# A convolution, an MLP and a scan on one core: the first stage's head and tail, its rows in DRAM, and the MLP's PSUM banks

## The chip, the core and the metric

The kernel runs on one core of a Trainium2 chip. Its time is device microseconds, the median of several runs. The profile is that of one execution. Engines are named as in the profile: PE multiplies matrices, DVE and ACT are the vector and scalar engines, POOL is GpSimd, SP only issues DMAs. ACT and POOL issue DMAs too.

## The reference

The input x is 32 images of 96 channels, 56 x 56, float32. Layer 0 is a depthwise 7x7 convolution, a LayerNorm over channels, a two-layer MLP with gelu, a scale and the residual. Layer 1 is a depthwise 5x5 convolution with silu and then a scan along the 3136 pixels. Cut to what matters:

```python
# layer 0
h = depthwise_conv7x7(x, conv_w) + conv_b           # then channels last
h = (h - mean(h)) * rsqrt(var(h) + 1e-5) * ln_g + ln_b
h = gelu(h @ w1 + b1) @ w2 + b2                      # 96 -> 384 -> 96
x = h * layer_scale + x
# layer 1
xs = silu(depthwise_conv5x5(x, conv_w) + conv_b)     # (B, 96, 3136)
dts, Bs, Cs = split(x_proj_w @ xs)                   # 6, 4, 4 rows
delta = softplus(dt_w @ dts + dt_b)
dA = maximum(delta * A, log(1e-9));  P = exp(cumsum(dA))
hs = P * cumsum(delta * Bs * xs / maximum(P, 1e-9))
y = einsum(hs, Cs) + xs * Ds
```

## The kernel before

The stages run one after the other on the core: the first convolution with the sums for the LayerNorm (0 to about 387 us of the profiled execution), the MLP with the residual (to about 1210), the second convolution (to about 1560) and the scan.

**First convolution.** There are 48 jobs. Each takes four pairs of a channel and a half of the image's rows (jobs 0 to 39: two channels, both halves; 40 to 43: four channels, upper half h = 0; 44 to 47: the lower half). `load_x(n)` brings a job's input `xt` in four DMAs of 224 KB, `load_taps(n)` its taps `wt` in four DMAs of 28 KB from `taps1_d`, a padded copy of the taps in DRAM that DVE builds in `pad` and a DMA stores first. `turn(n)` copies `wt` on ACT into one of three banded matrices `mats`. `convolve(n)` is 128 matmuls (line 380) into two of the four PSUM buffers of the pool `c1_ps`, each of two banks. `evict(n)` adds the bias on ACT (L408) and stores the result to `conv1_d` from ACT's queue (L414). `add_sums(n)` adds it to the running sums `acc1` on DVE (L430 to L436), and one job later its squares (ACT L439) to `acc2` (L441).

Loads run three jobs ahead, and `xt` and `wt` have four buffers each. Between the jobs, from n = 2 on, one function of the list `beside` runs in each turn: `first_weights` (folding the LayerNorm into w1: two small matmul groups in the PSUM buffers `ps_w1` and `ps_b1`), four times `first_rows` (copies of that result into `w1r_t`), `second_weights`, `scan_weights` (another small matmul, `ps_wd`), and the taps of the second convolution. `finish_norm(h)` makes 1/std of half h of the rows in five DVE operations, a Sqrt on ACT and a reciprocal on DVE; it is called for h = 0 at job `upper` = 44, for h = 1 in the MLP. POOL's queue stores its result to `rstd_d`. `load_rows(n)` loads a group's rows for the MLP: three tiles `h` of 4 rows x 32 channels, and the matching 1/std `r`. `normalise` multiplies them.

**Order.** An instruction inside `pin(...)` keeps its place in program order on its engine; one without it may be moved by the scheduler to where it judges its inputs ready. In the built kernel before, the unpinned SP loads are reordered: the taps `wt` of jobs 6 and 7 stand ahead of the input of job 6, from then on taps run two jobs further ahead than inputs; four loads of the first `h` tile stand among the loads of the jobs near 17 and four of the second among those near 33; the second convolution's taps store (L279) stands on SP as well. DMAs issued from SP and ACT take turns on eight completion semaphores, and one that takes a semaphore waits for the DMA that used it last.

**MLP.** 28 groups of rows, two halves each (`parts` = 56). In each, `hidden` (L520, into `ps_h`, three PSUM buffers of two banks) and gelu (L530), then `result` (L539, into `ps_o`, two buffers of one bank), the residual on DVE (L553), and a store to `block_d` from POOL's queue (L564). Rows and residual inputs are loaded two groups ahead.

**Second convolution and scan.** They read `block_d` (L625) and `conv2_d`; the scan runs units of four operations on DVE (L825 to L832), three on ACT (L809 to L811) and two on POOL (L815, L844).

## Time and profile before

| | |
|---|---|
| runs, us | 3349.49, 3348.69, 3347.18 (median 3348.69) |
| profiled execution, us | 3343.99, its span 3342.2 |
| busy share of the span | PE 83%, DVE 78%, ACT 67%, POOL 50% |
| mean granted PE clock | 0.819 |
| first convolution matmul | 17.90 us |
| first MLP matmul, first gelu | 387.18 us, 393.44 us |
| DMA | 788.08 MB, 236 GB/s over the span |
| row loads h<-conv_d | 336 DMAs of 112 KB, 2.6 us to landing |

Times within the execution are from its start. A bracket after an instruction gives how long its engine had been idle before it, and what released it; "DMA wt<-taps_d" is the DMA that wrote wt from the taps in DRAM. PEld is PE's weight load; SPq, ACTq and POOLq are the issuing of DMAs by those engines. In the profile, buffer and tensor numbers are left out: `conv_d` is conv1_d in the first stage, `taps_d` is taps1_d or taps2_d.

### The profile page before, as it was taken

The page shows a single profiled execution, that of the slowest core. Times are in us where ns is not written, and L with a number is a line of the kernel's source. Part 1 is how long each engine was busy: PE and PEld are TensorE (multiplying, and loading weights), DVE is VectorE, ACT ScalarE, POOL GpSimd, SP SyncE. Part 2 cuts the span into 40 slices and gives each one's busy share as a digit, 9 for nine tenths or more (in the row PEclk, how much of TensorE's full clock was granted, in tenths as well). Part 3 has the DMA queues.
Part 4 walks back from the last instruction along what each step waited for, and adds up shares of the span by engine and source line. Part 5 has one row for each costly group of instructions (what it writes and reads, how often), then busy time and mean ns, then how long its engine had stood idle before and what let it go on. Part 6 is the DMA issues. An engine that isn't in the chain of part 4 may idle for free. (4 is left out here: it accounts for less than half of the span.)

```text
span 3342.2 us, 54129 instructions
## 1 busy us (share of the span) xinstructions
PE 2775.9 (83%) x21898; PEld 1064.9 (32%) x21898; DVE 2599.4 (78%) x1538; ACT 2241.5 (67%) x1963; POOL 1686.6 (50%) x815
## 2 busy tenths in 40 slices
PE   5999899999999989997677777777777777777775
PEld 2566433333333333343222222222222222222221
DVE  4888743333333349997799999999999999999998
ACT  3566543333333348786888887888888888878784
POOL 1000101010010100000899898989899998989896
PEclk8999899999999999998666666666666666666767
DMA  7899856555565459998887877878787878778773
GB/s 188 262 304 293 237 152 182 149 166 163 150 183 145 129 142 278 285 289 226 293 296 246 284 258 272 261 271 277 257 280 248 291 250 283 255 273 264 269 267 113
DMA packets 303130, 788.08 MB, mean 236 GB/s; under 512 B 125680, under 2 KB 195952, under 8 KB 278336
## 3 DMA queue, kind: packets, MB, share of 16 engines
q1 hardware_dynamic: 266832, 659.81, 62.9%
q10 hardware_dynamic: 27200, 82.59, 6.6%
q0 software_dynamic: 8848, 42.23, 4.5%
q8 instruction: 172, 2.82, 0.4%
q14 instruction: 78, 0.64, 0.1%
HBM read 543.58 MB, written 240.90 MB: 235 GB/s over the span
## 5 line engine op out<-in xcount | busy, mean ns | idle before, releaser
L815 POOL TENSOR_TENSOR rep<-rep,bt 128x1568 f32<-128x1568 f32 x192 | 674.5, 3513 | 380.4 <-DMA rep<-du_d 380.4
L844 POOL TENSOR_TENSOR hs<-hs,ct 128x1568 f32<-128x1568 f32 x191 | 669.4, 3505 | 98.6 <-DVE hs L832 87.2
L825 DVE TENSOR_TENSOR_SCAN pv<-rep,pv 128x1568 f32<-128x1568 f32 x192 | 664.4, 3461 | 40.0 <-ACT rep L811 23.0
L530 ACT ACTIVATE g<-ph,b1p_t 128x896 f32<-128x896 f32 x336 | 319.9, 1003 | 483.0 <-PE ph L520 483.0
L553 DVE SCALAR_TENSOR_TENSOR o<-po,b2r_t,x 128x224 f32<-128x224 f32 x336 | 190.8, 609 | 529.9 <-PE po L539 523.1
L564 POOL DMA_DIRECT2D block_d<-o x168 | 81.2, 490 | 727.5 <-DVE o L553 622.4
L520 PE MATMUL ph<-h,w1r_t 32*128 32x448 f32 x4032 | 430.2, 554 | 5.9 <-ACT hs L408 4.2
L743 PE MATMUL pz<-xs,wd_t 96*96 96x392 f32 x512 | 275.3, 703 | 172.6 <-ACT du L751 128.0
L539 PE MATMUL po<-g,w_t 128*32 128x448 f32 x4032 | 413.0, 543 | 0.0
L862 PE MATMUL py<-hs,sel_t 128*32 128x392 f32 x1536 | 324.9, 673 | 61.8 <-POOL hs L844 61.6
L790 PE MATMUL pk<-bn,pick_t 8*128 8x392 f32 x1024 | 289.0, 685 | 93.5 <-ACT y L871 80.4
L828 DVE SCALAR_TENSOR_TENSOR pv<-pv,rep 128x1568 f32<-128x1568 f32 x192 | 345.6, 1800 | 21.7 <-POOL rep L815 1.8
L380 PE MATMUL ps<-xt,mat 32*64 32x432 f32 (+2 forms) x6144 | 320.9, 564 | 45.2 <-ACT mat L362 38.4
L832 DVE TENSOR_TENSOR_SCAN hs<-rep,carry_h,pv 128x1568 f32<-128x1568 f32 x96 | 334.1, 3480 | 10.0
L660 DVE COPY st<-yt 28x896 f32<-28x896 f32 x288 | 323.3, 1123 | 22.7 <-ACT yt L651 12.7
L637 PE MATMUL ps<-xq,wt 128*32 128x448 f32 x3072 | 307.2, 546 | 38.6 <-DMA xq<-block_d 29.3
L832 DVE TENSOR_TENSOR_SCAN hs<-rep,pv 128x1568 f32<-128x1568 f32 x96 | 328.4, 3420 | 9.6
L810 ACT ACTIVATE rep<-rep,lift_t 128x1568 f32<-128x1568 f32 x192 | 307.6, 1602 | 6.2
L811 ACT ACTIVATE rep<-rep,lift_t 128x1568 f32<-128x1568 f32 x192 | 307.6, 1602 | 6.3
L809 ACT ACTIVATE rep<-rep,a_t 128x1568 f32<-128x1568 f32 x192 | 308.3, 1606 | 1.8 <-DMA rep<-du_d 1.4
L854 PE MATMUL py<-xs,dsm_t 96*96 96x392 f32 x512 | 299.7, 726 | 10.0 <-ACT ct L794 4.5
L520 PEld LDWEIGHTS ph<-h,w1r_t 32*128 32x128 f32 x4032 | 192.3, 185 | 245.5 <-issue 153.0
(110 smaller groups left out, 2795.6 us busy)
## 6 DMA issues: line engine op xcount, KB each, us to landing
rep<-du_d SPq DMA_DIRECT2D x191, 1568.0 KB, 8.2
du_d<-du SPq DMA_DIRECT2D x126, 588.0 KB, 9.2
xq<-block_d SPq DMA_DIRECT2D x192, 225.0 KB, 5.1
xt<-in_x_dram SPq DMA_DIRECT2D x192, 224.0 KB, 4.6
block_d<-o POOLq DMA_DIRECT2D x168, 240.0 KB, 4.9
h<-conv_d SPq DMA_DIRECT2D x336, 112.0 KB, 2.6
x<-in_x_dram SPq DMA_DIRECT2D x336, 112.0 KB, 2.5
conv_d<-st SPq DMA_DIRECT2D x96, 392.0 KB
```

The costliest lines, as they stand in the source:

```text
L380: nc.tensor.matmul(pss[k // 2][2 * RW * p : 2 * RW * p + 2 * RW, k % 2, :HALF].rearrange("p (i r) -> p i r", r=W2)[:, :, lo:hi], lhsT=wv[r ...
L520: pin(nc.tensor.matmul(phs[i // 2][:, i % 2, :HALF], lhsT=w1r_t[rows, d, f * 128 : (f + 1) * 128], rhs=hts[n, d][rows, s * HALF : (s + 1) ...
L530: pin(nc.scalar.activation(gt, ph[:, :, :HALF], AF.Gelu, bias=b1p_t[:, f : f + 1], scale=1.0))
L539: pin(nc.tensor.matmul(po[CB * i : CB * i + CB, :HALF], lhsT=w2_t[:, f, CB * d : CB * d + CB], rhs=gts[n, s, f, i // 2][:, i % 2], start=( ...
L660: pin(copy(st[:, :, :, :, f], yt[RW * f : RW * f + QR].rearrange("p h (b q) -> p h b q", q=QW),))
L809: pin(nc.scalar.activation(da, da, AF.Exp, scale=a_t[:, g : g + 1]))
L815: pin(nc.gpsimd.tensor_mul(ut, ut, bts[i // NG]))
L825: pin(nc.vector.tensor_tensor_scan(grown, da, zero, pv[:, last : last + 1] if q else 1.0 / EPS, ALU.mult, ALU.add))
L828: pin(nc.vector.scalar_tensor_tensor(run, in0=grown, scalar=1.0, in1=ut, op0=ALU.min, op1=ALU.mult))
L832: pin(nc.vector.tensor_tensor_scan(ht, da, run, carry_h[:, col : col + 1] if q else 0.0, ALU.mult, ALU.add))
L844: pin(nc.gpsimd.tensor_mul(ht, ht, cts[k]))
L862: pin(nc.tensor.matmul(py[g * DG : (g + 1) * DG, s, :BK], lhsT=sel_t, rhs=hss[k * NG + g][:, cols], start=False, stop=True, tile_position= ...
```

## The change

- The DRAM tensor `conv1_d` is laid out by block of 32 channels, so that a tile `h` of 4 rows x 32 channels is loaded by one DMA of 448 KB in place of four of 112 KB. `block_d` is declared with two dimensions merged; its memory is as it was.
- At the head, the taps store and the first `wt` are issued by SP instead of ACT, the store ahead of the first input; a one-element copy `warm` on ACT comes first. POOL's loads of w1, ln_g, ln_b, b1 and two small matrices come before the other parameters.
- `first_weights`, all `first_rows` and the small matmul for `wd_t` run before the first job, in one PSUM buffer.
- All loads of inputs, taps, rows and 1/std are pinned. `load_rows(0)` is called at job 44 (before: 45), `load_rows(1)` after the last job. The reciprocal of `finish_norm(0)` comes ahead of job 44's sums on DVE.
- `rstd_d` is stored through SP instead of POOL, the second taps store through POOL instead of SP.
- The MLP's two PSUM pools are opened in the other order: `ps_o` takes the first two banks, `ps_h` the other six.

In the built program PE, DVE and ACT execute the same compute instructions but for one copy more on ACT; SP's order in the first stage becomes: input of job n, taps of job n, input of job n + 1, and so on, then the 1/std store, three h tiles, four r loads, and the same for group 1.

```diff
--- before.py
+++ after.py
@@ -80,8 +80,8 @@
 
 
 
-    conv1_d = [dram.tile([128, C, HALF], F32, name=f"conv1_{h}_d") for h in range(2)]
-    block_d = dram.tile([C, H, QC, B2, BI * QP], F32, name="block_d")
+    conv1_d = [dram.tile([C // CB, 128, CB, HALF], F32, name=f"conv1_{h}_d") for h in range(2)]
+    block_d = dram.tile([C, H, QC, B * QP], F32, name="block_d")
     conv2_d = dram.tile([C, H, B * W], F32, name="conv2_d")
     du_d = dram.tile([B * NCH, C, 2, CH], F32, name="du_d")
     rstd_d = [dram.tile([128, HALF], F32, name=f"rstd_{h}_d") for h in range(2)]
@@ -139,7 +139,7 @@
         pin(nc.scalar.activation(a2, a2, AF.Sqrt, bias=eps_t, scale=1.0))
         yield
         pin(nc.vector.reciprocal(a1, a2))
-        nc.gpsimd.dma_start(rstd_d[h], a1)
+        pin(nc.sync.dma_start(rstd_d[h], a1))
         yield
 
 
@@ -158,22 +158,17 @@
         h, row, p = group(n)
         for d in range(blocks):
             ht = inputs.tile([128, COLS], F32, name=f"h_{n}_{d}", tag="h", bufs=9)
-            for i in range(RB):
-                nc.sync.dma_start(
-                    two(ht[CB * i : CB * i + CB]),
-                    conv1_d[h].rearrange("(p s m) c q -> p m c s q", s=2, m=RW)[
-                        p, row + i, CB * d : CB * d + CB
-                    ],
-                )
+            rows = conv1_d[h][d].rearrange("(p s m) c q -> p (m c) s q", s=2, m=RW)
+            pin(nc.sync.dma_start(two(ht), rows[p, CB * row : CB * (row + RB)]))
             hts[n, d] = ht
         rt = inputs.tile([128, COLS], F32, name=f"r_{n}", tag="r")
         rts[n] = rt
         for i in range(RB):
             at = rstd_d[h][2 * RW * p + row + i, 0:1]
-            nc.sync.dma_start(
+            pin(nc.sync.dma_start(
                 two(rt[CB * i : CB * i + CB]),
                 bass.AP(at.tensor, at.offset, [[0, CB], [RW * HALF, 2], [1, HALF]]),
-            )
+            ))
 
     def normalise(n, d):
         pin(nc.vector.tensor_mul(hts[n, d], hts[n, d], rts[n]))
@@ -189,19 +184,20 @@
         ]
 
         kt1 = prep.tile([C, K1, K1], F32, name="kt1")
-        nc.sync.dma_start(kt1, c1w.rearrange("c (i j) -> c i j", j=K1))
+        pin(nc.sync.dma_start(kt1, c1w.rearrange("c (i j) -> c i j", j=K1)))
         xts: dict = {}
         wts: dict = {}
 
         def load_x(n):
             xts[n] = pool.tile([128, 2 * COLS], F32, name=f"xt1_{n}", tag="xt")
             for k, (c, h) in enumerate(jobs[n]):
-                nc.sync.dma_start(
+                pin(nc.sync.dma_start(
                     two(xts[n][RW * k : RW * k + RW]),
                     x[c].rearrange("(j m) q -> m j q", m=H)[h * (H - RW) : h * (H - RW) + RW],
-                )
-
-        load_x(0)
+                ))
+
+        warm = prep.tile([128, 1], F32, name="warm1")
+        pin(nc.scalar.copy(warm, eps_t))
 
         def column(src, n, name, pool=prep):
             t = pool.tile([n, 1], F32, name=name)
@@ -217,7 +213,8 @@
         pad = prep.tile([C, TP, K1], F32, name="pad1")
         nc.vector.memset(pad, 0.0)
         nc.vector.tensor_copy(pad[:, QR : QR + K1], kt1)
-        nc.scalar.dma_start(taps1_d, pad.rearrange("c p j -> c (p j)"))
+        pin(nc.sync.dma_start(taps1_d, pad.rearrange("c p j -> c (p j)")))
+        load_x(0)
 
         mats = [prep.tile([128, SJ, RW], F32, name=f"mat_{i}") for i in range(3)]
         for t in mats:
@@ -225,25 +222,25 @@
         for t in acc1, acc2:
             nc.vector.memset(t, 0.0)
 
-        c2b_t = across(c2b, 128, C, "c2b_t", const)
-        dtb_t = column(dtb, C, "dtb_t", const)
+        w1_t = prep.tile([C, F], F32, name="w1_t")
+        nc.gpsimd.dma_start(w1_t, w1)
         g_t = column(ln_g, C, "g_t")
         lnb_t = column(ln_b, C, "lnb_t")
+        b1_t = prep.tile([128, 3], F32, name="b1_t")
+        nc.gpsimd.dma_start(b1_t, b1.rearrange("(f p) -> p f", p=128))
+        xp_t = prep.tile([R, C], F32, name="xp_t")
+        nc.gpsimd.dma_start(xp_t, xp[:R, :])
+        dtwT_t = prep.tile([R, C], F32, name="dtwT_t")
+        nc.gpsimd.dma_start(dtwT_t, dtwT)
         b2_t = column(b2, C, "b2_t")
         ls_t = column(ls, C, "ls_t")
         ls_b = across(ls, 128, C, "ls_b")
+        nc.gpsimd.dma_start(w2_t, w2.rearrange("(f p) c -> p f c", p=128))
+        c2b_t = across(c2b, 128, C, "c2b_t", const)
+        dtb_t = column(dtb, C, "dtb_t", const)
         ds_t = column(ds, C, "ds_t")
-        w1_t = prep.tile([C, F], F32, name="w1_t")
-        nc.gpsimd.dma_start(w1_t, w1)
-        b1_t = prep.tile([128, 3], F32, name="b1_t")
-        nc.gpsimd.dma_start(b1_t, b1.rearrange("(f p) -> p f", p=128))
-        nc.gpsimd.dma_start(w2_t, w2.rearrange("(f p) c -> p f c", p=128))
-        xp_t = prep.tile([R, C], F32, name="xp_t")
-        nc.gpsimd.dma_start(xp_t, xp[:R, :])
         xpT_t = prep.tile([C, R + 2 * N], F32, name="xpT_t")
         nc.gpsimd.dma_start(xpT_t, xpT)
-        dtwT_t = prep.tile([R, C], F32, name="dtwT_t")
-        nc.gpsimd.dma_start(dtwT_t, dtwT)
         for g in range(NG):
             nc.gpsimd.dma_start(
                 a_t[:, g : g + 1],
@@ -276,7 +273,7 @@
                             pad2[:, k, RW - K2 : RW, f * 2 + t], turned[:, :, j]
                         )
             if k == QC - 1:
-                nc.sync.dma_start(taps2_d, pad2)
+                nc.gpsimd.dma_start(taps2_d, pad2)
 
         w1g = prep.tile([C, F], F32, name="w1g")
         held: dict = {}
@@ -286,15 +283,18 @@
             cen = prep.tile([C, C], F32, name="cen")
             kept(nc.vector.tensor_scalar, cen, ident[:C, :C], -1.0 / C, None, ALU.add)
             kept(nc.vector.tensor_scalar, w1g, w1_t, g_t, None, ALU.mult)
-            held["w1"] = bank("ps_w1")[:, 0]
+            ps = bank("ps_w1")
+            held["w1"], ps = ps[:, 0], ps[:, 1]
             nc.tensor.matmul(held["w1"][:C, :F], lhsT=cen, rhs=w1g, start=True, stop=True)
-            ps = bank("ps_b1")[:, 0]
             for f in range(3):
                 nc.tensor.matmul(
                     ps[:, f : f + 1], lhsT=w1_t[:, f * 128 : (f + 1) * 128], rhs=lnb_t,
                     start=True, stop=True,
                 )
             kept(nc.vector.tensor_add, b1p_t, ps[:, :3], b1_t)
+
+            held["wd"] = ps[:C, 256 : 256 + C]
+            nc.tensor.matmul(held["wd"], lhsT=xp_t, rhs=dtwT_t, start=True, stop=True)
 
         def first_rows(i):
             for d in range(C // CB):
@@ -315,10 +315,6 @@
                     )
 
         def scan_weights():
-
-            ps = bank("ps_wd")[:, 0]
-            nc.tensor.matmul(ps[:C, :C], lhsT=xp_t, rhs=dtwT_t, start=True, stop=True)
-            kept(nc.vector.tensor_copy, wd_t, ps[:C, :C])
             kept(nc.vector.tensor_scalar, dsm_t, ident[:C, :C], ds_t, None, ALU.mult)
             kept(nc.scalar.activation, a_t, a_t, AF.Exp)
             kept(nc.vector.tensor_scalar, a_t, a_t, -1.0, None, ALU.mult)
@@ -342,8 +338,7 @@
                 sel_t, ident.rearrange("p (d n) -> p d n", n=N), mybir.AxisListType.X, ALU.add
             )
 
-        beside = [first_weights] + [lambda i=i: first_rows(i) for i in range(RB)]
-        beside += [second_weights, scan_weights, scan_rows, turn_taps]
+        beside = [second_weights, scan_weights, scan_rows, turn_taps]
         beside += [lambda k=k: second_taps(k) for k in range(QC)]
 
         def load_taps(n):
@@ -351,10 +346,10 @@
             wt = pool.tile([128, RW * K1], F32, name=f"wt1_{n}", tag="wt")
             for k, (c, h) in enumerate(jobs[n]):
                 at = taps1_d[c, (1 - h) * R1 * K1 : (1 - h) * R1 * K1 + 1]
-                (nc.sync if n else nc.scalar).dma_start(
+                pin(nc.sync.dma_start(
                     wt[RW * k : RW * k + RW],
                     bass.AP(at.tensor, at.offset, [[K1, RW], [1, RW * K1]]),
-                )
+                ))
             wts[n] = wt
 
         def turn(n):
@@ -409,9 +404,10 @@
                         to, ps, AF.Identity, bias=c1b_t[:, ch : ch + 1], scale=1.0
                     ))
             for g in range(2) if n < whole else [h]:
-                cs = slice(c, c + 2) if n < whole else slice(c, c + JT)
+                d, at = divmod(c, CB)
+                cs = slice(at, at + 2) if n < whole else slice(at, at + JT)
                 of = slice(2 * g, 2 * g + 2) if n < whole else slice(0, JT)
-                pin(nc.scalar.dma_start(conv1_d[g][:, cs], hs[:, of]))
+                pin(nc.scalar.dma_start(conv1_d[g][d][:, cs], hs[:, of]))
             return hs
 
         def add_sums(n, hs):
@@ -446,8 +442,12 @@
         for n in range(1, 3):
             load_x(n)
             load_taps(n)
-        for n in range(2):
-            turn(n)
+        turn(0)
+        first_weights()
+        for i in range(RB):
+            first_rows(i)
+        kept(nc.vector.tensor_copy, wd_t, held["wd"])
+        turn(1)
         upper = whole + len(jobs[whole:]) // 2
         squares = None
         for n in range(len(jobs)):
@@ -464,8 +464,8 @@
             if n == len(jobs) - 2:
                 for d in range(blocks):
                     normalise(0, d)
+            next(norm, None)
             before, squares = squares, add_sums(n, hs)
-            next(norm, None)
             if n + 2 < len(jobs):
                 turn(n + 2)
 
@@ -476,9 +476,9 @@
                 squares = None
             if n >= 2 and beside:
                 beside.pop(0)()
-            if n == len(jobs) - 3:
+            if n == upper:
                 load_rows(0)
-                load_rows(1)
+        load_rows(1)
 
 
 
@@ -487,8 +487,8 @@
     with tc.tile_pool(name="mlp_g", bufs=14) as pool_g, tc.tile_pool(
         name="mlp_ot", bufs=1
     ) as pool_o, tc.tile_pool(name="mlp_x", bufs=9) as pool_x, tc.tile_pool(
-        name="mlp_h", bufs=3, space=PSUM
-    ) as ps_h, tc.tile_pool(name="mlp_o", bufs=2, space=PSUM) as ps_o:
+        name="mlp_o", bufs=2, space=PSUM
+    ) as ps_o, tc.tile_pool(name="mlp_h", bufs=3, space=PSUM) as ps_h:
         xts: dict = {}
         gts: dict = {}
 
@@ -562,7 +562,7 @@
                 m = (1 - h) * QR + row
                 for i in range(RB):
                     nc.gpsimd.dma_start(
-                        block_d[CB * d : CB * d + CB, m + i].rearrange("c k j q -> c (k j q)"),
+                        block_d[CB * d : CB * d + CB, m + i].rearrange("c k q -> c (k q)"),
                         ot[CB * i : CB * i + CB].rearrange("p k q -> p (k q)"),
                     )
 
@@ -621,10 +621,11 @@
             wts[c] = wt
             for h in range(2):
 
-                rows = block_d[c, (H - RW + 2) * (1 - h) : (H - RW + 2) * (1 - h) + RW - 2]
+                first = (H - RW + 2) * (1 - h)
+                rows = block_d[c, first : first + RW - 2]
                 pin(nc.sync.dma_start(
                     xqs[c % len(xqs)][h][2 * QC * h : 2 * QC * h + (RW - 2) * QC],
-                    rows.rearrange("m k j q -> (m k) (j q)"),
+                    rows.rearrange("m k q -> (m k) q"),
                 ))
 
         def convolve(c):
```

## The prediction

> **What bounds the kernel now.** I read the busy times by stage first (columns: length, busy time of PE, PEld, DVE, ACT, POOL, then granted clock, DMA share, GB/s).
>
> ```profile
> 38.40:55.00 16.60, 2.58 (x11) 1.94 (x12) 8.54 (x6) 6.11 (x6) 0.00 (x0) 0.60 0.83 230
> 55.00:112.60 57.60, 50.84 (x903) 22.12 (x902) 45.20 (x49) 25.61 (x26) 0.00 (x0) 0.94 0.68 205
> 112.60:324.00 211.40, 201.09 (x3980) 142.98 (x3988) 187.87 (x125) 122.70 (x124) 0.00 (x0) 0.99 0.97 292
> 324.00:387.00 63.00, 48.75 (x894) 35.04 (x877) 54.85 (x45) 34.62 (x48) 0.55 (x1) 0.89 0.88 266
> 900.00:1000.00 100.00, 100.00 (x992) 37.43 (x988) 33.84 (x52) 38.77 (x41) 11.59 (x24) 1.00 0.61 175
> 2300.00:2700.00 400.00, 305.90 (x1080) 95.84 (x1078) 386.66 (x134) 333.18 (x282) 367.76 (x140) 0.68 0.80 264
> ```
>
> The MLP (900:1000) is bound by PE alone, the scan (2300:2700) by DVE with POOL close behind. The change alters neither's compute. Only the first convolution, up to 387 us, has an idle PE. The timeline says where (start, duration, instruction, idle time before it and its releaser):
>
> ```profile
> 15.95 1.28 ACT L362 ACT_TABLE_LOAD   x1 [15.95 <-DMA wt<-taps_d]
> 17.90 20.48 PE L380 MATMUL ps<-xt,mat 32*64 32x448 f32 x384 [17.90 <-ACT mat L362]
> 52.41 1.56 PE L290 MATMUL ps_w<-w1g,cen 96*96 96x384 f32 x2 [14.04 <-DVE w1g L259]
> 54.98 9.04 PE L380 MATMUL ps<-xt,mat 32*64 32x448 f32 x132
> ...
> 72.02 6.53 PE L380 MATMUL ps<-xt,mat 32*64 32x448 f32 x128 [1.08 <-ACT hs L408]
> ...
> 112.62 44.22 PE L380 MATMUL ps<-xt,mat 32*64 32x448 f32 x892 [0.71 <-DVE wd_t L259]
> 160.23 8.15 PE L380 MATMUL ps<-xt,mat 32*64 32x448 f32 x128 [3.39 <-ACT mat L362]
> 197.19 44.53 PE L380 MATMUL ps<-xt,mat 32*64 32x448 f32 x896 [0.38 <-ACT mat L362]
> 316.94 37.88 PE L380 MATMUL ps<-xt,mat 32*64 32x448 f32 x768 [0.25 <-ACT mat L362]
> 361.53 8.66 PE L380 MATMUL ps<-xt,mat 32*64 32x448 f32 x128 [6.71 <-ACT mat L362]
> 373.71 9.28 PE L380 MATMUL ps<-xt,mat 32*64 32x448 f32 x128 [3.52 <-ACT mat L362]
> 387.18 6.34 PE L520 MATMUL ph<-h,w1r_t 32*128 32x448 f32 x28 [4.19 <-ACT hs L408]
> ```
>
> The reader is to see three kinds of idle PE: the wait for w1g (14.04), a small wait for an eviction in every job up to 112, and waits for ACT's matrix (mat) in the middle and at the end. A job is 128 matmuls. Undisturbed it takes 44.53 x 128/896 = 6.36 us. Jobs 0 to 2 start at 17.90, job 3 at 54.98, job 10 at 112.62, job 40 at 316.94; job 47 ends at 383.0.
>
> **The change part by part.** The sum is made against the profiled execution (span 3342.2, 3343.99 in all); the median shown, 3348.69, is 4.7 us above that, so gains are subtracted from the median.
>
> A. *Head.* ACT's first copy of taps waits until 15.95 for wt, then pays a 1.28 table load. The taps store still issues at 3.4 (DVE's pad copy ends at 3.39) and still takes 4.2 us until wt 0 may issue (7.60 to 9.39). But only four x DMAs lie ahead of wt 0 on SP, not eight, and a wt took 4.0 us to land (median of the first 60 us, DMA view): 13.4; the table is loaded by then; copy 0.6: 14.0. PE first runs the weights: w1's DMA issues at 3.4 to 3.9 on POOL instead of 8.06, +6.7 (its landing row) = 10.6, w1g 0.41, then 1.56 + 1.28 + gaps 0.4 + wd 0.40 = 14.6. Job 0 starts at 14.5: gain 3.4. Bounds: 5 if wt lands in 3, a loss of 1 if w1 still lands at 15. x 0 is issued 2.6 us later (SP waits on the pad copy with x 0 behind it); with a landing of 4.3 it is there by 10, ahead of taps.
>
> B. *Jobs 2 to 3.* PE waits 14.04 for w1g, which sits in DVE's order behind the sums, and its four matmuls end at 54.98: 38.38 to 54.98 is 16.6. All leave this place. The next thing late: the matrix of job 3 was copied at 38.34, that of job 4 only at 47.58, 3 us behind need, as ACT's store issue waited for an input load. Value 15; bounds 10 and 16.6.
>
> C. *Jobs 3 to 9.* ps_w stays in one of four PSUM buffers until DVE has made all 12 copies of w1r, four turns later, so each job waits for an eviction (1.08). 57.64 us went into seven jobs; at 6.4 they take 44.8: gain 12.8. The 12 copies (0.55 each, 6.7) and wd's 0.25 now run from about 14.6 to 21.5 on DVE, which has nothing until job 0's eviction (26 before). Job 1's second buffer is that one, free at 21.5, when job 0 ends at 21: nothing to pay; without that cover 6.9.
>
> D. *Jobs 10 to 39.* 204.3 us for 30 jobs, against 192 at 6.4. The losses sit at jobs 17 to 20 (3.39 idle at 160.23, then starts 9.0, 7.6 and 7.1 apart) and 33 to 36. There SP's order held the second conv's taps store (5.0 waiting on DVE, by SP's waits) and four row loads of h each time; both leave: the store to POOL, idle then, the rows behind the last input by pins. Value 12; bounds 5 and 14.
> Here the skill speaks against the change: "DMA: Bandwidth & Descriptors", Rules for kernel authors, says to issue a DMA early and wait late, so its fixed cost overlaps. By it the early row loads were right: D would be 0 and two loads (3.1 each by that page's 2.0 us + bytes/436 GB/s, an estimate) would come to the end, about 18 us off my sum. The trace shows ACT's copy waiting 8.9 us in two waits on h<-conv_d, mid-stage, and at the end the rows are not last: 1/std is. I take the row.
>
> E. *Job 40 to the first gelu*, 316.94 to 393.44. Jobs 40 to 45 run to 354.8 as before. The matrix of job 46 stands behind the forced squares and Sqrt on ACT. Before, job 44's store issue waited until 358.66 for SP's row loads; now nothing does (SP and ACT share eight completion semaphores in program order, so a store may wait for an earlier SP load). Finish ends on DVE at 357.8, Sqrt 0.67, copy 0.6: job 46 starts at 359.0, cold, 8.7, to 367.7. Reciprocal 2.94 now precedes job 44's sums: 361.4; rstd is on SP then, with only row loads and x of the MLP behind it. It lands at 365.2 (3.8 was POOL's landing), r (2.9) by 369. Job 45's store uses a semaphore after rstd's: ACT waits until 365.2, then copies job 47's matrix at 365.8, still in time. Job 47 ends at 374. Of the two ends of this part, before:
>
> ```profile
> 358.66 0.33 ACTq L414 DMA_DIRECT2D conv_d<-hs  x1
> ...
> 368.90 3.59 SPq L173 DMA_DIRECT2D r<-rstd_d  x8
> ...
> 393.44 1.91 ACT L530 ACTIVATE g<-ph,b1p_t 128x896 f32<-128x896 f32 x2
> ```
>
> the first is the late store issue, the second the 1/std rows that SP could issue only then, with ACT's next store behind them on a shared semaphore (372.63), the third the first gelu. DVE needs to 369.8 for job 45's sum, 372 for squares, 375.2 for normalise (3.09). In the new bank order the first ph needs banks of job 46, not 47, so the 4.19 goes. ACT: evict 47, Square 46 behind DVE's sum at 379.4, 1.7, table 1.28: first gelu 382.4. Gain 11; bounds 4 and 14 (if DVE lags less).
>
> F. *Row loads in the MLP.* 336 DMAs of 112 KB become 84 of 448 KB. The same page (Anatomy of one DMA) gives a fixed 2.0 us each: 252 x 2.0 = 504 us, as an estimate. The row is PE 100.00 of 100.00 busy: h comes two turns ahead, so this is 0. What if the cover were gone: a later landing of 4.7 instead of 2.6, some 2 us once. The new row layout leaves row pieces and bytes as they are, and block_d is the same memory under other names: 0. rstd 1 on SP waits for DVE at part 5, with part 6's rows behind it, which have 29 us to spare: 0.
>
> Sum: 3.4 + 15 + 12.8 + 12 + 11 = 54.2; 3348.7 - 54.2 = 3294.5.
>
> **The rivals.**
> *DMA takes PE's place.* A job moves 0.92 MB in, 0.92 out and 0.11 of taps: 1.95 MB, 6.67 us at the 292 GB/s of 112.6:324. With DMA share 0.97 that may be the pace. Then C is 10.9 and D 4.2, B 12: 3.4 + 12 + 10.9 + 4.2 + 11 = 41.5, and with a further 10 lost in filling the queue at the head about 31: 3307 to 3318. Against: 197 to 242 ran seven jobs without an idle PE at 6.36.
> *The pinned loads wait on the stores (slower).* Before, wt ran two jobs further ahead of its input on SP. Now wt n+3 comes directly behind x n+3, and its last DMA reuses the semaphore of job n-1's store, so SP waits for that to land, and the next inputs queue behind. Loop from the end of job n-1 to job n+3: evict 1.9, issue 0.8, landing 5.4, issue 0.9, wt landing 4.9, a turn on ACT 2.7, copy 0.6: 17.2 us against three jobs, 19.1. Each 3 us over costs 1 per job. It decides where the pace passes 7.5 (48 x 7.5 + 14.5 = 374.5, plus the end's 8 gives the old 383): landings summing to 15.6 instead of 10.3 (6.9 of the loop is other work). At 17 the loop is 23.9, the pace 8.0, job 47 ends at 48 x 8.0 + 22.5 = 406.5: 24 us slower, 3372. Against: the medians, under a DMA share of 0.97.
> *It doesn't do what it says at the head*: weights land as late as before, PE's in-order queue then holds job 0 to 20: 5.5 less, 3300, inside the main case.
>
> **How the numbers follow.** Main case (gain 42 to 66) 0.68; DMA pace or a partial loss (gain 7 to 42) 0.22; within 0.2% (6.7 us, about what a measurement of this kernel tells from no change) 0.03; slower 0.07. Predicted 3294.5. The low end, 3278, is a gain of 70: the upper bounds of A, B, D and E with C make 62.4, and a pace 0.2 us shorter over the 37 jobs of C and D, 7.4 more (320 to 340 us held 418 matmuls in 20.00 busy us: 6.12 a job). The high end, 3320, takes in the DMA case (gain 29); the slow case and partial losses beyond stay outside, about 0.15 with the tail below.
>
> **What would show it.** Right: first convolution matmul near 14.5 with four weight matmuls ahead of it; no PE wait on w1g or w1r; job 3 near 35, job 10 near 80; no h load before 300; 84 h DMAs; first ph near 320 to 328 without a wait on evictions; later stages of unchanged length. Wrong: ACT's mat copy waiting on wt with jobs over 7 us, DMA share at 1 with PE idle between jobs, or an MLP with PE below 99%.

## The result, and the profile after

The changed kernel took 3312.69 us (median of 4 runs, 3307.17 to 3314.3) against 3348.76 (4 runs on the same chip): a ratio of 0.989, 95% interval 0.9873 to 0.9907, or 36 us less. The forecast was 54 us less, 3294.5, with 3278 to 3320 as the range. The profiled execution took 3313.1 us (span 3311.2), 30.9 less than that of before; the terms below are read from these two.

First the busy times by stage, in the columns that the prediction gave (length, busy time of PE, PEld, DVE, ACT, POOL, granted clock, DMA share, GB/s). The stages are cut at the new starts of jobs 3, 10 and 40 and at the first gelu.

```profile
15.00:39.20 24.20, 21.54 (x384) 8.91 (x384) 13.90 (x16) 6.00 (x9) 3.19 (x6) 1.00 0.86 216
39.20:86.40 47.20, 45.68 (x898) 31.10 (x898) 44.25 (x59) 28.16 (x30) 0.00 (x0) 1.00 0.96 291
86.40:289.00 202.60, 193.96 (x3842) 136.99 (x3842) 183.27 (x102) 120.04 (x121) 0.52 (x1) 1.00 0.98 295
289.00:361.00 72.00, 60.14 (x1052) 41.23 (x1052) 64.92 (x51) 42.69 (x55) 0.00 (x0) 0.91 0.85 261
900.00:1000.00 100.00, 100.00 (x992) 37.09 (x988) 32.52 (x50) 39.71 (x42) 5.80 (x12) 1.00 0.50 149
2300.00:2700.00 400.00, 304.31 (x1069) 95.35 (x1062) 386.78 (x134) 335.37 (x283) 364.50 (x141) 0.68 0.80 270
```

The last two rows are much as before: the MLP is full of PE, the scan of DVE. The third is the surprise: 30 jobs still take 202.6 us, with DMA share 0.98 and 295 GB/s. PE's timeline after the change, with the same columns as before's:

```profile
9.04 1.59 PE L288 MATMUL ps_w<-w1g,cen 96*96 96x384 f32 x2 [9.04 <-DVE w1g L256]
10.43 1.28 PE L290 MATMUL ps_w<-lnb_t,w_t 96*128 96x1 f32 x6
13.29 0.60 PE L297 MATMUL ps_w<-dtwT_t,xp_t 6*96 6x96 f32 x2 [1.58 <-DMA dtwT_t<-in_dtwT_dram]
15.42 21.54 PE L375 MATMUL ps<-xt,mat 32*64 32x448 f32 x384 [1.53 <-ACT mat L357]
39.23 6.60 PE L375 MATMUL ps<-xt,mat 32*64 32x448 f32 x128 [2.28 <-ACT mat L357]
...
86.36 19.04 PE L375 MATMUL ps<-xt,mat 32*64 32x448 f32 x384 [0.17 <-ACT mat L357]
107.24 6.60 PE L375 MATMUL ps<-xt,mat 32*64 32x448 f32 x128 [1.84 <-ACT mat L357]
115.05 6.59 PE L375 MATMUL ps<-xt,mat 32*64 32x448 f32 x128 [1.21 <-ACT mat L357]
...
288.99 32.02 PE L375 MATMUL ps<-xt,mat 32*64 32x448 f32 x640 [0.21 <-ACT mat L357]
321.16 6.59 PE L375 MATMUL ps<-xt,mat 32*64 32x448 f32 x128 [0.16 <-ACT mat L357]
331.44 8.20 PE L375 MATMUL ps<-xt,mat 32*64 32x448 f32 x128 [3.68 <-ACT mat L357]
344.36 8.53 PE L375 MATMUL ps<-xt,mat 32*64 32x448 f32 x128 [4.72 <-ACT mat L357]
355.20 4.97 PE L520 MATMUL ph<-h,w1r_t 32*128 32x448 f32 x28 [2.31 <-ACT hs L403]
```

The weights now stand ahead of job 0 and the waits on w1g and on w1r are gone. What is left are waits for ACT's matrix: one before job 3, many small ones from job 3 to job 40, and two large ones at the end. ACT's timeline shows what is behind the last:

```profile
331.29 2.19 ACT L403 ACTIVATE hs<-ps,c1b_t 128x448 f32<-128x448 f32 x4
343.27 0.33 ACTq L410 DMA_DIRECT2D conv_d<-hs  x1
343.72 0.59 ACT L357 COPY mat<-wt 128x224 f32<-128x224 f32 x1 [10.23 <-DMA r<-rstd_d]
...
360.79 1.90 ACT L530 ACTIVATE g<-ph,b1p_t 128x896 f32<-128x896 f32 x2
```

The first row is the eviction of job 45, the second its store, issued only when a load of 1/std rows had landed; ACT sat idle for 10.23 us behind it, with job 47's matrix next. The first gelu comes at 360.79 instead of 393.44. SP had issued the loads of these rows from 335.97 on, behind three loads of `h`:

```profile
334.31 1.56 SPq L162 DMA_DIRECT2D h<-conv_d  x3
335.97 1.82 SPq L168 DMA_DIRECT2D r<-rstd_d  x4
```

From the first gelu to the end it is 2950.4 us against 2948.8 before.

### The profile page after: what moved, and what is told of

Same layout as the page of the kernel before. It is cut to its first block, busy times and chain, and to the rows that moved or that the text cites. A ratio compares the mean times of both kernels' runs of the same rounds, so it can differ in the third digit from the quotient of the medians.

```text
span 3311.2 us, 53717 instructions
## 1 busy us (share of the span) xinstructions
PE 2783.1 (84%) x21898; PEld 1078.3 (33%) x21898; DVE 2593.7 (78%) x1538; ACT 2240.1 (68%) x1964; POOL 1685.9 (51%) x814
```

## The experiments

"D" below is the time from the start of job 10 to that of job 40, "pace" the mean from job 3 to job 40, "E" the time from the start of job 40 to the first gelu. Starts inside an unbroken group of matmuls are interpolated. Ratios are to the kernel before on the same chip. D, pace and E each come from one profiled execution. Two of the kernels below (old order of the PSUM pools, stores of jobs 45 to 47 from POOL) have the changed kernel's code up to job 44, and their D was 200.7 and 199.4 against 202.6, so some 3 us of D is scatter between executions.

### What sets the pace: DMA rate or the order of the queues

**All stores from POOL.**

```diff
-                pin(nc.scalar.dma_start(conv1_d[g][d][:, cs], hs[:, of]))
+                pin(nc.gpsimd.dma_start(conv1_d[g][d][:, cs], hs[:, of]))
```

> The changed kernel, with the first convolution's results stored from POOL's queue instead of ACT's. No byte is moved less; a store no longer takes a completion semaphore of the ring that SP's loads use, and ACT issues no DMA in this stage. Bytes theory (DMA rate sets the pace of jobs 10 to 40): jobs 10 to 40 still take about 202 us (6.7 a job), DMA share stays above 0.95; only the end gains, since ACT's copy of job 47's matrix has no store ahead of it: 4 to 5 us, about 3308. Order theory (waits on shared semaphores set the pace): jobs 10 to 40 fall to about 192 us (6.4 a job), and with the end about 3297.

Measured: 3296.68 us, ratio 0.9849 (0.9836 to 0.9863). D is 194.5, pace 6.47, E 67.7. PE's timeline begins with 21 jobs in one group:

```profile
15.11 134.58 PE L375 MATMUL ps<-xt,mat 32*64 32x448 f32 x2688 [1.30 <-ACT mat L357]
149.93 6.59 PE L375 MATMUL ps<-xt,mat 32*64 32x448 f32 x128 [0.24 <-ACT mat L357]
156.72 51.30 PE L375 MATMUL ps<-xt,mat 32*64 32x448 f32 x1024 [0.21 <-ACT mat L357]
```

The same bytes went through faster, at 303 GB/s in 112 to 289 us against 294 of the changed kernel there. So 294 GB/s was no limit of the DMA engines, though their share was 0.98. The order theory's numbers nearly came out (192 and 3297 forecast); the bytes theory's did not. The wait before job 3 went as well (job 3 starts at 34.34).

**Half of the stores' bytes.**

```diff
-                pin(nc.scalar.dma_start(conv1_d[g][d][:, cs], hs[:, of]))
+                half = slice(64 * g, 64 * g + 64)        # jobs 0 to 39
+                pin(nc.scalar.dma_start(conv1_d[0][d][half, cs], hs[half, :2]))
-            rows = conv1_d[h][d].rearrange(...)
+            rows = conv1_d[0][d].rearrange(...)
```

> The changed kernel, with half of the bytes of the stores of jobs 0 to 39 left out: the two DMAs per job remain on the same queue in the same order, but each writes 64 partitions of the upper half's rows; the lower half's rows are not stored and the MLP reads the upper half's twice, so its output is another. A job moves 1.49 MB instead of 1.95. Bytes theory: at 290 GB/s that is 5.1 us, under PE's 6.36, so PE sets the pace: jobs 10 to 40 take about 192 us instead of 202.6, and jobs 3 to 10 lose 2 more; about 3299. Order theory: semaphores are taken in the same order, only the landings of the stores get shorter; jobs 10 to 40 stay above 199 us, about 3309.

Measured: 3292.56 us, ratio 0.9836 (0.9822 to 0.985); D 187.5, pace 6.26. Taken alone this looks like proof of the bytes theory. With the run above it is not: fewer bytes also shorten every landing (inputs 4.4 us in 112 to 289 instead of 5.0), and a loop of waits made of landings shortens with them. The run did not separate the two, which I had not seen when I wrote what to expect. It settles another question: SP issued the same eight DMAs a job here, so the time that SP takes to issue them is not what held the pace at 6.75.

**Matrix copy ahead of the stores.**

```diff
+            if n + 2 < len(jobs):
+                turn(n + 2)
+            keep(n, hs)          # the two store issues, taken out of evict
```

> The changed kernel, with ACT's copy of the taps into the matrix of job n+2 placed ahead of the issue of job n's stores instead of behind it. Nothing else moves. Bytes theory: the pace of jobs 10 to 40 stays near 6.7 us (about 202 us in all); at the end job 47's matrix is copied at about 334 instead of 343.7, so job 47 follows job 46 at once, 4.7 us earlier, and the first gelu comes at about 356: in all about 3308. Order theory: ACT's copy behind its own blocked store issue was the wait that set the pace, so jobs 10 to 40 fall to 192 to 195 us and the whole to about 3298.

Measured: 3317.76 us, ratio 0.9916 (0.9901 to 0.9932); D 212.1, pace 7.02, slower than the changed kernel. Both theories missed. The first eight jobs run unbroken, but now ACT's square stands behind the store and waits instead. ACT's waits in 112 to 289 us (what waited, for what, total, times, longest):

```profile
ACT dt L438 <- DMA xt<-in_x_dram: 42.2, 15, 3.3
ACT dt L438 <- issue: 12.1, 3, 5.2
```

The store waits for an input load wherever it stands on ACT, and since it is issued later, what it holds up on SP comes later too: SP's taps loads waited 8.0 us for stores to land in 112 to 310, against 3.2 in the changed kernel. The wait was moved and enlarged, not removed.

**Taps two jobs further ahead.**

```diff
-                load_taps(n + 3)
+            for m in (3, 4, 5) if n == 0 else (n + 5,):
+                if m < len(jobs):
+                    load_taps(m)
```

> The changed kernel, with the taps loaded two jobs further ahead (job n issues the input of n+3 and the taps of n+5; four taps buffers still suffice). Same DMAs, same queues, same number per turn of the ring. Lead theory: ACT's copy of the matrix never waits for taps, jobs 10 to 40 fall from 202.6 to about 192 us, and the whole to about 3301. Ring theory: a store still takes the semaphore of an input load eight DMAs back and the taps that of a store, so the pace stays within 6.5 to 6.75 us and the time within 4 us of 3312.

Measured: 3314.11 us, ratio 0.9906 (0.9891 to 0.9922); D 197.8, jobs 3 to 10 in 50.6 instead of 47.1. The last 20 jobs before job 46 ran in one group at 6.41, yet the extra taps at the start cost what was gained. The lead is worth at most a few us of D, near the scatter; the pace over all, 6.71, stays in the ring theory's range.

**Taps from POOL.** This takes four of the ten DMAs of a job out of the ring of semaphores and leaves ACT's queue as it is.

```diff
-                pin(nc.sync.dma_start(
+                pin((nc.gpsimd if n > 2 else nc.sync).dma_start(
                     wt[RW * k : RW * k + RW],
```

> The changed kernel, with the taps of jobs 3 to 47 loaded from POOL's queue instead of SP's. Stores stay on ACT's queue, between the same instructions as before; bytes are the same. Only the ring changes: per job it holds four input loads and two stores instead of ten DMAs, so a store takes the semaphore of an input load of the job before, long landed. Ring theory: jobs 3 to 40 run near PE's 6.41 us, jobs 10 to 40 in about 193 to 196 us instead of 202.6, and the whole is about 3300 to 3304 (the end stays as in the changed kernel). Rival (what slows the changed kernel is ACT's queue itself: a store issue of about 0.8 us and its waits ahead of the matrix copy): pace stays at 6.6 to 6.75, 198 to 202 us, about 3310.

Measured: 3302.5 us, ratio 0.9862 (0.9843 to 0.988); D 189.8, and from job 13 on 33 jobs in one group, 6.25 us each:

```profile
104.33 206.12 PE L375 MATMUL ps<-xt,mat 32*64 32x448 f32 x4224 [0.88 <-ACT mat L357]
```

It moved 317 GB/s in 112 to 289 us, more than any other version. SP's waits from 112 to 310 us tell why, first of the changed kernel, then of this one:

```profile
SPq L194 <- DMA wt<-taps_d: 34.0, 29, 2.2
SPq L194 <- DMA xt<-in_x_dram: 28.0, 25, 1.7
...
SPq L349 <- DMA conv_d<-hs: 3.2, 7, 0.7
```

```profile
SPq L194 <- PE ps L375: 70.1, 30, 3.5
SPq L194 <- DMA conv_d<-hs: 62.1, 32, 3.7
```

In the changed kernel an input's issue waits for earlier taps and inputs to land, that is for their semaphores. Here it waits for PE to free the buffer (70.1 us) and for earlier stores to land (62.1), yet PE waits for nothing: loads have run ahead, and PE is the bound. The single landings are longer here than in the changed kernel (stores 6.5 us against 4.9, inputs 5.5 against 5.0), and the pace is better all the same. Jobs 3 to 12 took 6.66 each. The second taps store blocked POOL for 25.4 us, until 95 us, with the taps of job 13 behind it, but PE stood only 0.88 us before job 13; in 37 to 104 the weight loads waited 24.0 us in 99 short waits for nothing that the profile shows, and why is open.

**How long the ring holds a job.** In my expectations I had named one loop of waits, of about 13.4 us for two jobs, from a store's landing through taps and input to the next store. The waits above do not show that loop: taps waited for a store only 3.2 us in all. What they show is the ring as a whole, an issue waiting for whichever earlier DMA holds its semaphore, mostly inputs behind taps and inputs. Its size follows from the landings of the changed kernel in 112 to 289 us (count, size, median us to landing):

```profile
conv_d<-hs ACTq DMA_DIRECT2D x54, 448.0 KB, 4.9
xt<-in_x_dram SPq DMA_DIRECT2D x106, 224.0 KB, 5.0
wt<-taps_d SPq DMA_DIRECT2D x104, 28.0 KB, 4.9
```

A job's two stores, four inputs and four taps hold a semaphore for 49.4 us together. On eight semaphores that is, as an estimate, at least 6.2 us a job; at the measured 6.7, on average 7.4 of the eight are taken, so the ring was nearly full all the time. The same estimate for the other versions, from their own landings:

| version | DMAs of a job in the ring | least time per job, us | pace, us |
|---|---|---|---|
| changed kernel | 10 | 6.2 | 6.75 |
| all stores from POOL | 8 (inputs 5.7, taps 6.0) | 5.9 | 6.47 |
| half of the stores' bytes | 10 (4.6, 4.4, 4.3) | 5.5 | 6.26 |
| taps from POOL | 6 (6.5, 5.5) | 4.4 | 6.36 (6.25 from job 13 on) |

Where the estimate comes well under 6.25 PE sets the pace; where it comes near or over, the ring does. A landing itself grows when more is moving, so the DMA engines have a part in the 4.9 to 5.0 us; how large a part, no run here shows.

**How much PE was waiting where the timeline shows none.** The waits of PE's weight load: first of the kernel before in its best stretch, the seven jobs of 197 to 242 us, then of the changed kernel and of the version with all stores from POOL, both in 230 to 280 us:

```profile
PEld ps L380 <- ACT mat L362: 4.6, 7, 1.1
```

```profile
PEld ps L375 <- ACT mat L357: 5.1, 7, 1.5
```

```profile
PEld ps L375 <- ACT mat L357: 4.8, 8, 1.2
```

With taps from POOL no such wait is left in 230 to 280. So the "undisturbed" jobs of these stretches had a wait of the weight load at about every job, which the timeline joins over; a job that waits for nothing takes 6.25. A late matrix is not the only such wait: the first 21 jobs of the version with all stores from POOL also took 6.41 each, with 3.5 us of waits for a matrix in 34 to 150 us and 28.5 us, in 159 short waits, for nothing that the profile shows.

### The parts of the change alone

**Only part D, on the kernel before.**

```diff
-                nc.sync.dma_start(taps2_d, pad2)
+                nc.gpsimd.dma_start(taps2_d, pad2)
-                nc.sync.dma_start(two(ht[...]), ...)      # and the loads of r
+                pin(nc.sync.dma_start(two(ht[...]), ...))
```

> The kernel before, with only the prediction's part D applied: the second convolution's taps store goes from SP to POOL, and the row loads of the MLP are pinned in program order. Taps still run two jobs further ahead of inputs on SP, as before. Lead theory (the changed kernel stays at 6.75 us a job because wt n+3 comes directly behind x n+3): here the taps keep their lead, so jobs 10 to 40 fall from 204.3 to 192 to 194 us, a gain of 10 to 12. Ring theory (eight completion semaphores shared by SP's loads and ACT's stores tie the stores to the loads at about 13.4 us for two jobs, wherever the taps stand): the disturbances near jobs 17 and 33 go, but the pace stays at 6.5 to 6.75, 196 to 202 us, a gain of 2 to 8.

Measured: 3339.86 us, ratio 0.9979 (0.9971 to 0.9988), 7 us less. D is 195.9 instead of 204.3, between the two theories' ranges. The two disturbances near jobs 17 and 33 are gone, and jobs 20 to 40 ran at 6.42. So what the prediction named as the loss is a loss, of 8.4 us, give or take the 3 us of scatter, where the taps keep their lead.

**Only the head, on the kernel before.** The diff is that of the change from `kt1` to `second_weights` and of the calls ahead of the first job, with pins on the first input and the first taps alone.

> The kernel before, with only the head of the change: taps store and the first taps from SP, one-element copy on ACT, POOL's parameter order, weights in one PSUM buffer with the small wd matmul, all folded ahead of the first job. Inputs and taps from job 1 on, the second taps store and the row loads are left to the scheduler as before. By the prediction's terms A, B and C as measured in the changed kernel (2.5, 13.3, 10.5): job 10 starts near 86 instead of 112.6, and the whole gains 26, about 3321. Rival (the freed PE only meets the loop of loads and stores earlier): job 10 near 86, but jobs 10 to 40 longer than 204, whole gain under 20.

Measured: 3324.75 us, ratio 0.9935 (0.9922 to 0.9947), 21.7 less (17.7 to 26.1) rather than 26. Job 10 starts at 90.4, D is 206.2. Part of the rival holds: jobs 3 to 10 take 51.3, and the loop is met earlier.

**MLP's PSUM pools in the old order.**

```diff
-        name="mlp_o", bufs=2, space=PSUM
-    ) as ps_o, tc.tile_pool(name="mlp_h", bufs=3, space=PSUM) as ps_h:
+        name="mlp_h", bufs=3, space=PSUM
+    ) as ps_h, tc.tile_pool(name="mlp_o", bufs=2, space=PSUM) as ps_o:
```

> The changed kernel, with the MLP's two PSUM pools in their old order. If the prediction was right that the new order gives the first hidden matmul banks of job 46 instead of job 47, its start falls back behind the last eviction by some 2 to 4 us and the whole is 3 us slower, about 3316. If the new order only exchanges one buffer of job 47 for its other one (banks 2 and 3 for 0 and 1), the first hidden matmul waits 2.3 us for the last eviction in both, and the time stays within the scatter of 3312.7.

Measured: 3309.69 us, ratio 0.9882 (0.9864 to 0.99), the same as the changed kernel's. The first hidden matmul waits as long with the old order as with the new one (2.31, above):

```profile
351.86 4.97 PE L520 MATMUL ph<-h,w1r_t 32*128 32x448 f32 x28 [2.30 <-ACT hs L403]
```

By the built kernels job 47 fills banks 2 and 3 with its first half and banks 0 and 1 with its second; the first hidden matmul takes banks 2 and 3 in the new order, 0 and 1 in the old (no trace shows the banks). In both it is released by the last of job 47's four evictions, which in the changed kernel run from 352.94 to 355.15. This part of the change does nothing here that can be measured.

**Rows in four DMAs again.**

```diff
-            rows = conv1_d[h][d].rearrange("(p s m) c q -> p (m c) s q", s=2, m=RW)
-            pin(nc.sync.dma_start(two(ht), rows[p, CB * row : CB * (row + RB)]))
+            for i in range(RB):
+                pin(nc.sync.dma_start(two(ht[CB * i : CB * i + CB]), ...))
```

> The changed kernel, with conv1_d in the old layout and each h tile loaded by four DMAs of 112 KB instead of one of 448 KB, pinned in the same place. Theory (the loads are covered by PE in the MLP): MLP between 500 and 1200 us unchanged to 1 us, PE busy 100.00 of 100.00 in 900 to 1000. At the end of the first stage more DMAs share the ring ahead of the 1/std rows and job 45's store: first gelu 0 to 4 us later. In all 3312 to 3317. By the skill's fixed cost of about 2.0 us a DMA (DMA: Bandwidth & Descriptors, Anatomy of one DMA) 252 more DMAs would cost up to 504 us, an estimate, if they were not covered.

Measured: 3312.76 us, ratio 0.9891 (0.9875 to 0.9907), the same. The MLP has PE full in both, though in 400 to 1200 us an h load lands in 2.6 us here and in 4.6 in the changed kernel, and a 1/std row in 3.1 and 6.3:

```profile
500.00:600.00 100.00, 100.00 (x992) 36.88 (x984) 33.67 (x51) 40.01 (x42) 11.59 (x24) 1.00 0.54 162
```

The fixed 2.0 us per DMA of the Trainium skill ("DMA: Bandwidth & Descriptors", Anatomy of one DMA) would make 504 us of the difference, as an estimate. The page fits that figure on GpSimd's path; the prediction and this run's expectation carried it over to SP's loads, for which no run here gives a fixed cost. Behind PE the difference is nothing that this measurement tells from zero.

### The end of the stage

**Stores of jobs 45 to 47 from POOL.**

```diff
+                queue = nc.gpsimd if n > upper else nc.scalar
-                pin(nc.scalar.dma_start(conv1_d[g][d][:, cs], hs[:, of]))
+                pin(queue.dma_start(conv1_d[g][d][:, cs], hs[:, of]))
```

> The changed kernel, with only the stores of jobs 45 to 47 issued from POOL's queue. Theory of the end (job 45's store waits on ACT for a semaphore that the loads of h and r hold, and job 47's matrix stands behind it): that copy comes at about 334 instead of 343.7, PE's idle 4.72 before job 47 goes, job 47 ends near 346, first gelu at 354 to 356 instead of 360.8, in all about 5 us less than the changed kernel, 3308. Rival (1/std sets the end: Sqrt, reciprocal, its store, r's landing, normalise): job 47 comes earlier but the first gelu stays within 2 us of 360.8, and the time within 2 us of 3312.7.

Measured: 3304.24 us, ratio 0.9876 (0.9858 to 0.9894), some 5 us less than the changed kernel by the two ratios, whose intervals overlap; the profiles give 4.2 of it to E (67.6 against 71.8). ACT's timeline:

```profile
327.60 0.61 ACT L357 COPY mat<-wt 128x224 f32<-128x224 f32 x1
...
348.13 1.70 ACT L436 ACTIVATE dt<-dt 128x1792 f32<-128x1792 f32 x1 [5.84 <-DVE acc L433]
```

The copy of job 47's matrix follows the eviction of job 45 at once and job 47 follows job 46 without an idle PE. The next thing late is ACT's square of job 46, which stands ahead of the first gelu (351.14) and waits for DVE's sums; these stood behind the normalise, which waited for the 1/std rows.

**Sums of job 46 ahead of the normalise, on top of all stores from POOL.**

```diff
-            if n == len(jobs) - 2:
-                for d in range(blocks):
-                    normalise(0, d)
             next(norm, None)
             before, squares = squares, add_sums(n, hs)
+            if n == len(jobs) - 2:
+                for d in range(blocks):
+                    normalise(0, d)
```

> The kernel with all stores of the first convolution from POOL, and in addition DVE's normalise of the first rows placed behind the sums of job 46 instead of ahead of them. In the first of these the normalise waits for 1/std until 331 with the sums of job 46 behind it, and ACT's square of job 46 (338.4 to 340.1) and the table load stand ahead of the first gelu at 341.4. With the sums first: sums at 329 to 333.2, square to 335, normalise 333.2 to 336.3, first gelu at 337 to 338: 4 us less, about 3293. Rival: first gelu is bound by 1/std and the first ph, not by the square: no change, 3297.

Measured: 3297.27 us, ratio 0.9854 (0.9838 to 0.987): no change against 3296.68. The first gelu came at 337.4, as forecast, but 2.6 us of the 4 came from jobs 40 and earlier; E fell from 67.7 to 66.3 only. The square was done at 332.5, but the first hidden matmul now waited 3.16 us for DVE's normalise, which stands behind those sums: DVE's work in a row had become the last.

**The combination.** Taps from POOL with the second taps store moved behind the taps of job 23, the last three stores from POOL, and the order of the sums.

> The version that the runs point to: the changed kernel with the taps of jobs 3 to 47 loaded from POOL, the stores of jobs 45 to 47 issued from POOL, the second taps store pinned behind the taps of job 23 (where it stood, POOL waited 25.4 us for the last copy of pad2 with the taps of job 13 behind it), and DVE's normalise behind the sums of job 46. Ring theory: jobs 3 to 40 at 6.25 to 6.3 us as in the unbroken part of the version with taps from POOL (there 33 jobs in 206.12 us): job 40 starts at 36 + 37 x 6.27 = 268; the end as with all stores from POOL, 66 us: first gelu near 334, about 18 us ahead of the changed kernel's end in all beyond its own, 3290. Rival (at 6.25 us a job 1.95 MB is 312 GB/s, more than the 302 of the version with all stores from POOL, and DMA then sets the pace): job 40 at 274, first gelu near 340, 3297.

Measured: 3293.86 us, ratio 0.9845 (0.9832 to 0.9859). It beats the changed kernel (0.9873 to 0.9907) and, by intervals, only equals all stores from POOL (0.9836 to 0.9863). Job 40 starts at 271.9, first gelu at 337.1, E 65.2, pace 6.37: between the forecast and its rival. It moved 313 GB/s. Up to 162 us its jobs took 6.46 each, from there to job 46 6.27; PE's weight loads waited 36.5 us in 36 to 162, and 12.4 in 162 to 310, for nothing that the profile shows. Why it did not hold 6.25 is open.

## Why the prediction was right and wrong, by its terms

The changed kernel is faster, inside the range, but 18 us short of the sum. By the prediction's own chances its 36 us are the second case (gain 7 to 42, at 0.22) and not the main one (0.68). The range took the result in because its high end was set by the DMA rival, which had the size right but not the cause; that is partly luck. Term by term, from the two profiled executions (us):

| term | forecast | measured |
|---|---|---|
| A head, start of job 0 | 3.4 | 2.5 (17.90 to 15.42) |
| B jobs 0 to 3 | 15 | 13.3 (37.08 to 23.81) |
| C jobs 3 to 10 | 12.8 | 10.5 (57.64 to 47.13) |
| D jobs 10 to 40 | 12 | 1.7 (204.32 to 202.63) |
| E job 40 to first gelu | 11 | 4.7 (76.5 to 71.8) |
| F and the rest | 0 | -1.7 |
| sum | 54.2 | 31.0 |

**A** was right in mechanism. The weights end at 13.9, before the 14.6 forecast, and the matrix set the start: it was copied at 14.78 with the table already loaded, and job 0 started at 15.42, 0.9 after the forecast.

**B and C** were right: both waits left with their cause and the cover on DVE held (no wait on w1r). A wait of 2.28 before job 3 took part of B, as ACT's copy stood behind its store. C ran at 6.73 a job, not 6.4; that is the error of D again.

**D is the step that failed.** The prediction found the two disturbances rightly; alone they gave 8.4. It then set all 30 jobs to PE's pace of 6.4, because seven had run so without an idle PE. But that stretch had no slack: the weight loads waited seven times in those seven jobs for a matrix just copied. The ring of eight semaphores, with ten DMAs a job in it, stood ahead of PE, and the jobs took 6.75. The step needed the pace of the loads and took that of PE; 30 jobs at 0.35 us make 10.5, which is what D lacks (12 forecast, 1.7 measured, up to 5 by the other two executions of the same code). With six DMAs a job left in the ring (taps from POOL) D is 189.8, better than the 192 of the forecast.

**The rival "DMA takes PE's place"** had the right size (6.67 a job, 3307 to 3318) from the wrong cause. It read 292 GB/s at share 0.97 as a limit; the same work ran at 303, 313 and 317. **The slower rival** was nearer to the cause: it had the shared semaphores and the taps directly behind the input. But the wait that it built on, taps waiting for a store, came to 3.2 us, where inputs waited 62.0 for taps and inputs. Its loop came to 17.2 us for three jobs, within PE's 19.1, and so the semaphores were given no cost at all below its point of decision, 7.5 us a job, which was not reached.

**Signs.** Of the prediction's signs of being wrong two came: DMA share near 1 with PE idle between jobs, and ACT's copy waiting for taps (in 112 to 310 us), though at 6.7 and not over 7 us a job:

```profile
ACT mat L357 <- DMA wt<-taps_d: 74.0, 28, 3.8
```

The first hidden matmul came at 355.20 and behind an eviction, not at 320 to 328 without one. That sign was too early even by the prediction's own terms: job 47's end at 374, less the 43.2 of A to D, is 330.8.

**E** was mis-sized in three places. The 1/std rows were to land in 2.9 us; issued from 335.97 on behind h loads of 448 KB, the one that ACT's store waited for landed just before 343.27, some 7 us later. Job 45's store was to use a semaphore that came free with 1/std itself; it had that of this row load, so ACT waited 10.23 us, PE 4.72 before job 47. Issuing those stores elsewhere gives back 4.2. Job 46 started 3.7 us after job 45, near the 4.2 of the forecast. The bank swap, counted there as the end of a 4.19 wait, is nothing: 2.31 of that wait is left, and with the old order 2.30.

**F** was right: 252 fewer DMAs are worth nothing behind a full PE (3312.76 us with them, 3312.69 without). Where the other 1.7 us went is not settled. In the versions above, the time from the first gelu to the end lies between 2950 and 2956 us, so the difference is no larger than the scatter there.

The early row loads, for which the prediction had the rule "issue early, wait late" against it ("DMA: Bandwidth & Descriptors", Rules for kernel authors), were rightly kept out: taking them and the second taps store out of SP's middle together gave 7 us on the kernel before. The run does not part the two. SP's waits of before, in 80 to 340 us, name the store as the larger: it stood once for 5.0 us until DVE had its data, with all loads behind it, while the row loads (L162) waited 2.5 in all, and for semaphores rather than for their rows:

```profile
SPq L279 <- DVE pad L259: 5.0, 1, 5.0
...
SPq L162 <- DMA xt<-in_x_dram: 1.9, 3, 1.0
SPq L162 <- DMA conv_d<-hs: 0.6, 1, 0.6
```

So the rule's "early" has a price in this kernel: each early load takes a place in the ring, and an issue whose data are not yet there holds the queue for all behind it.

## What to carry to other kernels

A DMA share near 1 is not a limit until another order of the same bytes fails to move them faster; ask first what each issue waits for, count which loads and stores share completion semaphores, and divide their landing times by the number of semaphores. Take the pace of an "undisturbed" stretch only after reading the waits of PE's weight load in it, since the timeline joins over small ones. When two streams tie each other in a ring, issue one of them from another queue rather than reorder within the ring: reordering moved the wait, and either move, of the stores or of the taps, raised the pace.

## What the runs showed of the hardware that was not expected

- Single landings became longer while the whole became faster: with taps from POOL a store took 6.5 us instead of 4.9 and an input 5.5 instead of 5.0, at 317 GB/s instead of 294.
- POOL issued a store's DMA in 0.54 us and a taps load in 0.50 (medians of 112 to 289 us), where ACT took 0.33 for a store and SP 0.44 for a taps load; DVE's subtraction (L426) took 2.03 us with POOL's issues beside it and without.
- A job's 128 matmuls take 6.25 us when no wait is shown, 6.36 to 6.41 in stretches that look unbroken but have short waits of the weight load, and 6.59 behind a visible wait.
